# Scores of two heads from one 256-column product over zero-padded keys, in a graph layer on one core

## The chip, the cores and the metric

The kernel runs on one core of one Trainium2 chip, in one launch. The metric is the device time of that launch in microseconds (us). The core's engines each work through a queue of their own and meet at semaphores: TensorE (PE in the profile, with PEld for its weight loads), VectorE (DVE), ScalarE (ACT), GpSimd (POOL) and SyncE (SP, which here only issues DMAs).

## The reference

The kernel computes one layer of a graph network over 8192 nodes of 256 channels and 131072 edges that are sorted by their destination, and a layer norm:

```python
ea  = edge_attr @ w_e + b_e                       # 131072 x 64 -> 256
msg = relu(x[src] + ea)
agg = segment_sum(msg, dst, num_segments=8192)
h_local = bn1(relu((x + agg) @ w1 + b1) @ w2 + b2 + x)
qkv = x.reshape(256, 32, 256) @ in_w.T + in_b      # graphs of 32 nodes
q, k, v = split(qkv), 4 heads of 64 channels each
scores = einsum('bhqd,bhkd->bhqk', q, k) / 8
o = einsum('bhqk,bhkd->bhqd', softmax(scores), v)
h_attn = bn2(o @ out_w.T + out_b + x)
out = h_local + h_attn
out = bn3(out + relu(out @ m_w1 + m_b1) @ m_w2 + m_b2)
return layernorm(x + out)
```

Everything is float32. The change concerns `scores`: for each graph of 32 nodes and each of four heads, the products of 64-channel queries and keys.

## The kernel before

The work has two halves that run side by side.

**Edges.** The 131072 edges are 128 blocks of 1024. For each block POOL issues eight gathers (`gather`, line 205): indirect DMAs that fetch 128 rows of `x` each, into a tile `xs` of four rotating buffers. From block 20 on (`NX`) they fetch from `xb`, a copy of `x` with the edge bias added, which is made in the meantime by DVE (`copy_stream`, line 770) and stored by SP. PE multiplies the edge attributes with `we` (`edge_products`, tile `pe`, two PSUM tiles of two banks each); DVE adds the gathered rows (`edge_messages`, line 280), ACT applies the relu (line 284). PE then sums the messages into windows of nodes (`group_sums`, tile `pw`) and places them (`edge_place`, tile `l`), and DVE adds the result to the transposed node features `xT` (line 351). Before block 20 the bias is added on PE, by a product of the one-row selector `sel` with `be`.

**Nodes.** The nodes are 16 chunks of 512. `attention_front` transposes a chunk, and computes queries and keys (four products of 128 output channels x 512 nodes into PSUM tiles `at`, four banks in all), which ACT moves to the tile `qk` with the bias (line 519). `attention_back` computes the values (`at<-inT,xT`), the scores (lines 541 to 557), the softmax, the weighted values and the output projection. `dense` does the rest, when all edges of the chunk are placed; for the last chunk `dense_rows` does it in pieces of 128 nodes, with `diag` (the identity scaled by the last batch norm `s3`) and `c3row` (its bias as rows). These two are made at block 12, together with the scaling of `mw2`.

In the scores each head has 64 channels, so `qk` holds two heads in its 128 partitions. For each pair of heads and each group of 128 nodes there are two products over 64 partitions each, one for the upper and one for the lower half of the array; their 128 columns go to two different PSUM banks of one `pe` tile, the same tiles that the edge products use:

```python
matmul(two[:, s, a : a + P],
       qk[s * DH : (s + 1) * DH, hh, a : a + P],
       qk[s * DH : (s + 1) * DH, KC + hh, a : a + P], start=True, stop=True)
```

ACT then copies the four diagonal 32 x 32 squares (line 557) to `pr`. The page of the profile counts two instructions for each float32 product.

**Order.** PE's order is that in which the code is written (`manual_schedule`): the loop over blocks asks a planner (`Work`) for pieces of node work, by the costs that the `yield`s give. DVE and ACT follow the written order up to block 24 and are ordered by the compiler's scheduler after that. The gathers are issued in order, and `hold_fetches` lets each wait for a product of PE that the plan puts some 10 us earlier (`AHEAD`; in the tail from block 104 on, by `TAIL_LATE`), so that a PE that falls behind its plan by more than that holds the gathers back.

Of the kernel before, what the change touches and what calls it, by code (L numbers as in the profile page):

```python
# [9 lines left out]
FP = mybir.dt.float32  # L10
I32 = mybir.dt.int32
AF = mybir.ActivationFunctionType
# [6 lines left out]
P = 128  # L19
N, C, E, ED, H, NPG = 8192, 256, 131072, 64, 4, 32  # L20
DH = C // H
KC = C // P
# [11 lines left out]
CH = 512  # L34
NCH = N // CH
BPC = NB // NCH
TN = CH // P
# [7 lines left out]
AHEAD = 10.0  # L45
LATE = 12.0
TAIL_LATE = 9.9
STARTS = [4.8, 7.5, 13.2, 17.0, 20.5]
TE = 1
RS = 1.0 / (1.0 + 1e-5) ** 0.5  # L50
# [27 lines left out]
def gnn_kernel(ctx: ExitStack, tc: tile.TileContext, x, src, dst, edge_attr, w, out):  # L78
    nc = tc.nc

    const = ctx.enter_context(tc.tile_pool(name="const", bufs=1))
# [12 lines left out]
    ident = const.tile([P, P], FP, name="ident")  # L94
# [5 lines left out]
    eps_t = const.tile([P, 1], FP, name="eps_t")  # L100
    nc.vector.memset(eps_t, LN_EPS)

    sel = const.tile([P, P], FP, name="sel")
    nc.vector.memset(sel, 0.0)
    for h in range(2):
        nc.vector.memset(sel[h * ED : h * ED + 1, :], 1.0)
# [9 lines left out]
    be = const.tile([P, C], FP, name="be")  # L116
# [10 lines left out]
    for v in VECS:  # L127
        n = w[v].shape[0] // P
# [3 lines left out]
    def v_(name, i=0, n=1):  # L132
        return vec[:, col[name][0] + i : col[name][0] + i + n]
# [4 lines left out]
    s3 = const.tile([P, KC], FP, name="s3")  # L138
    s12 = const.tile([P, KC], FP, name="s12")
    cA = const.tile([P, KC], FP, name="cA")  # L140
    c3 = const.tile([P, KC], FP, name="c3")
    diag = const.tile([P, KC, P], FP, name="diag")
    c3row = const.tile([P, C], FP, name="c3row")

    fast = ExitStack()
    epool = fast.enter_context(tc.tile_pool(name="edge", bufs=1))
# [3 lines left out]
    def bank():  # L150
        return pps.tile([P, CH], FP, name="at", tag="at", bufs=4)

    def bank2():
        return pps.tile([P, 2, CH], FP, name="pe", tag="pe", bufs=2)
# [10 lines left out]
    def matmul(ps, *args, **kw):  # L165

        mark(ps, nc.tensor.matmul(ps, *args, **kw).ins)  # L167
# [192 lines left out]
    with tc.tile_pool(name="setup", bufs=1) as sp:  # L360
# [15 lines left out]
        for v in VECS:  # L376
            r, n = col[v]
# [7 lines left out]
        for h in range(NH):  # L385
            ps = bank()[:, : TJ * NB].rearrange("p (j s) -> p j s", j=TJ)
# [14 lines left out]


        nc.vector.memset(bd, 0.0)

        def turned(rows, cols, no):
            for o in range(0, no, 2):
# [8 lines left out]
        ps = bank()[:, :nrows]  # L415
# [30 lines left out]
        for h in range(0, NH, 2):  # L446
            ps2 = bank2()
            for i in range(2):
                ps = ps2[:, i, : TJ * NB].rearrange("p (j s) -> p j s", j=TJ)
# [34 lines left out]
        ps = bank()[:, : 2 * NB].rearrange("p (i s) -> p i s", i=2)  # L484
# [10 lines left out]
    def attention_front(n0, st, pool, bank):  # L495
        if "xn" not in st:
            load_nodes(n0, st, pool)
            yield REST
        xn = st["xn"]
        xT = st["xT"] = pool.tile([P, KC, CH], FP, name="xT", tag="xT", bufs=4)  # L500
        hA = st["hA"] = pool.tile([P, KC, CH], FP, name="hA", tag="hA", bufs=4)
        for k in range(KC):
            ps = bank()
            for t in range(TN):
                turn(ps[:, t * P : (t + 1) * P], xn[:, t, k * P : (k + 1) * P], ident)
            nc.scalar.copy(xT[:, k, :], ps)  # L506
            nc.scalar.activation(
                hA[:, k, :], xT[:, k, :], AF.Identity, scale=s12[:, k : k + 1], bias=cA[:, k : k + 1]
            )
        yield 0.9  # L510

        qk = st["qk"] = pool.tile([P, 2 * KC, CH], FP, name="qk", tag="qk")
        for o in range(2 * KC):
            ps = bank()
            for k in range(KC):
                matmul(
                    ps, inT[:, k, o * P : (o + 1) * P], xT[:, k, :], start=(k == 0), stop=(k == KC - 1)
                )
            nc.scalar.activation(qk[:, o, :], ps, AF.Identity, bias=v_("in_b", o))
            st["front"] = o == 2 * KC - 1  # L520
            yield 1.7

    def attention_back(st, pool, bank, bank2):
        xT, hA, qk = st["xT"], st["hA"], st["qk"]
        vn = pool.tile([P, TN, C], FP, name="vn", tag="vn")
        for t0 in range(0, TN, 2):
            ps = bank()
            for t in range(t0, t0 + 2):
                for k in range(KC):
                    matmul(  # L530
                        ps[:, (t - t0) * C : (t - t0 + 1) * C],
                        xT[:, k, t * P : (t + 1) * P],
                        inT[:, k, 2 * C :],
                        start=(k == 0),
                        stop=(k == KC - 1),
                    )
            nc.vector.tensor_copy(vn[:, t0 : t0 + 2, :].rearrange("p t c -> p (t c)"), ps)
            st["v"] = t0 + 2 == TN
            yield 1.7

        pr = pool.tile([P, TN, H, NPG], FP, name="pr", tag="pr")
        for hh in range(H // 2):
            two = bank2()
            for t in range(TN):
                for s in range(2):
                    a = t * P
                    matmul(
                        two[:, s, a : a + P],
                        qk[s * DH : (s + 1) * DH, hh, a : a + P],
                        qk[s * DH : (s + 1) * DH, KC + hh, a : a + P],  # L550
                        start=True,
                        stop=True,
                    )
            two4 = two.rearrange("p s (t k) -> p s t k", t=TN)
            for g in range(GT):
                q = slice(g * NPG, (g + 1) * NPG)
                nc.scalar.copy(pr[q, :, 2 * hh : 2 * hh + 2, :].rearrange("p t s k -> p s t k"), two4[q, :, :, q])
        st["scores"] = True
        yield 1.8
        prf = pr.rearrange("p t h k -> p (t h k)")  # L560
        pr3 = pr.rearrange("p t h k -> p (t h) k")
        mx = pool.tile([P, TN * H], FP, name="mx", tag="mx")
        nc.vector.tensor_reduce(mx, pr3, AX.X, ALU.max)
        parts = [slice(a, a + H) for a in range(0, TN * H, H)]
        for q in parts:
            nc.vector.tensor_sub(pr3[:, q], pr3[:, q], mx[:, q, None].to_broadcast([P, H, NPG]))
        nc.scalar.activation(prf, prf, AF.Exp, scale=1.0 / DH**0.5)
        yield PAUSE if stated[0] else 0.0
        sm = pool.tile([P, TN * H], FP, name="sm", tag="sm")
        nc.vector.tensor_reduce(sm, pr3, AX.X, ALU.add)  # L570
        nc.vector.reciprocal(sm, sm)
        for q in parts:
            nc.vector.tensor_mul(pr3[:, q], pr3[:, q], sm[:, q, None].to_broadcast([P, H, NPG]))

        for g in range(GT):
            q = slice(g * NPG, (g + 1) * NPG)
            nc.vector.transpose(bd[q, :, :, g, :].rearrange("p t h q -> p (t h) q"), pr3[q])  # L577
        yield REST
        oT = pool.tile([P, KC, CH], FP, name="oT", tag="oT")
        for k in range(KC):  # L580
            ps = bank()
            for t in range(TN):
                for s in range(2):
                    h = 2 * k + s
                    matmul(
                        ps[s * DH : (s + 1) * DH, t * P : (t + 1) * P],
                        vn[:, t, h * DH : (h + 1) * DH],
                        bd[:, t, h].rearrange("p g q -> p (g q)"),
                        start=True,
                        stop=True,  # L590
                    )
            nc.scalar.activation(oT[:, k, :], ps, AF.Identity, bias=v_("in_b", 2 * KC + k))
        yield 1.8
        for o in range(KC):
            ps = bank()
            for k in range(KC):
                matmul(
                    ps, outT[:, k, o * P : (o + 1) * P], oT[:, k, :], start=(k == 0), stop=(k == KC - 1)
                )
            nc.vector.scalar_tensor_tensor(  # L600
                hA[:, o, :], ps, s2[:, o : o + 1], hA[:, o, :], op0=ALU.mult, op1=ALU.add
            )
            st["done"] = o == KC - 1
            yield 1.7
# [244 lines left out]
    with tc.manual_schedule(engines={PE}):  # L849
# [9 lines left out]
        for c in range(NCH):  # L859
            st, before, same = chunk[c], chunk[c - 1], chunk[c - 4]  # L860
# [48 lines left out]
        b = 0  # L909
        while b < TAIL:  # L910
# [12 lines left out]

            if b == 12:
                ps = bank()[:, : 2 * C].rearrange("p (i c) -> p i c", i=2)
                for i, cols in enumerate((s3, c3)):
                    for k in range(KC):
                        nc.tensor.transpose(
                            ps[:, i, k * P : (k + 1) * P], cols[:, k : k + 1].to_broadcast([P, P]), ident
                        )  # L930
                nc.vector.tensor_mul(mw2, mw2, ps[:, 0, None, :].to_broadcast([P, 2 * KC, C]))
                nc.vector.tensor_copy(c3row, ps[:, 1, :])
                for k in range(KC):
                    nc.vector.tensor_scalar(diag[:, k], ident, s3[:, k : k + 1], None, ALU.mult)
            if stated[0]:
# [49 lines left out]
        t, l, s = came[b - 2] + 20, b - 2, b - 2  # L985
        p, m = [b, 0], [b, 0]
# [206 lines left out]
```

## Time and profile before

| | |
|---|---|
| median of 3 runs (lowest to highest) | 1314.71 us (1314.67 to 1316.24) |
| the profiled execution | 1313.67 us, span 1311.9 us |
| mean granted TensorE clock | 0.961 |
| PE, PEld, DVE, ACT, POOL busy | 92%, 55%, 61%, 45%, 74% of the span |
| DMA | 240.38 MB in 148926 packets, 183 GB/s |
| PE in the chain that ended last | 69% |

The span runs from the first to the last instruction of the profiled execution; some 2 us of its time lie outside. Rows of a timeline give start, duration, engine, line, operation, what it writes and reads, and in brackets the idle time before it with what ended it. Rows that group instructions give their count, busy time, the mean of one in ns, and the idle time before them. Rows of waits read: who waited for whom, total us, times, the longest in us. PE's spans overlap their successors a little, since the ends of matmuls are modelled: the distance from one start to the next is the better measure.

### The profile page before, as it was taken

How to read it: one execution, taken by the hardware profiler on the slowest of the kernel's cores; microseconds unless marked ns; L12 is line 12 of the kernel's file. 1: busy time of each engine (PE TensorE's matmuls, PEld its weight loads, DVE VectorE, ACT ScalarE, POOL GpSimd, SP SyncE). 2: the span in 40 equal slices, each digit the busy share in tenths (PEclk: the TensorE clock that was granted, in tenths of full speed). 3: DMA queues.
4: the chain of work that ended last, by engine and by line, in shares of the span. 5: the costliest groups of instructions: out<-in, count | busy, mean ns of one | idle time of the engine just before them, and what ended most of it. 6: DMA issues, size and time to landing. Idle time of an engine off the chain costs nothing.

```text
span 1311.9 us, 21686 instructions
## 1 busy us (share of the span) xinstructions
PE 1201.6 (92%) x7671; PEld 725.8 (55%) x7671; DVE 797.5 (61%) x1630; ACT 584.8 (45%) x840; POOL 975.2 (74%) x1032
## 2 busy tenths in 40 slices
PE   5997999999979979799798998989899799999997
PEld 3564555555546555555555555555555555556576
DVE  6675856757447465475745746465474665766563
ACT  2543434545435354253543536444263443545343
POOL 6777777777777777777777777777777777777772
PEclk9998999999989989899898998989999899999999
DMA  9999976766557665665666666566566665757552
GB/s 228 289 315 288 300 210 162 202 159 193 158 157 190 161 187 160 162 183 157 187 170 163 174 168 185 157 183 170 155 187 163 179 182 137 201 154 185 153 153 62
DMA packets 148926, 240.38 MB, mean 183 GB/s; under 512 B 27950, under 2 KB 112204, under 8 KB 148044
## 3 DMA queue, kind: packets, MB, share of 16 engines
q0 software_dynamic: 49152, 134.28, 37.7%
q1 hardware_dynamic: 98572, 104.65, 28.9%
q8 instruction: 62, 1.02, 0.3%
q14 instruction: 52, 0.43, 0.1%
q10 hardware_dynamic: 1088, 0.00, 0.0%
HBM read 222.06 MB, written 16.78 MB: 182 GB/s over the span
## 4 chain that ended last, share of the span: by engine, by line
PE 69%; DMA 10%; DVE 7%; issue 7%; POOL 4%; ACT 1%; SPq 0%; DVEq 0%; POOLq 0%
PE at L167 36%; PE pe L167 17%; PE pw L167 8%; DMA xs<-xb,srci 6%; PE l L167 5%; POOL xs L205 4%; DVE msg L280 3%; DMA xs<-in_x_dram,srci 2%; DVE bd L577 1%; PE at L703 1%; PE at L654 1%; DMA ea<-in_edge_attr_dram 1%; DVE eaT L239 1%; ACT msg L284 1%; PE at L171 1%
## 5 line engine op out<-in xcount | busy, mean ns | idle before, releaser
L205 POOL DMA_INDIRECT xs<-xb,srci x864 | 819.6, 949 | 263.2 <-issue 177.0
L284 ACT ACTIVATE msg<-msg 128x1024 f32<-128x1024 f32 (+1 forms) x259 | 270.7, 1046 | 466.7 <-DVE msg L280 465.6
L280 DVE TENSOR_TENSOR msg<-pe,xs 128x1024 f32<-128x1024 f32 (+1 forms) x259 | 310.3, 1208 | 250.6 <-DMA xs<-xb,srci 179.2
L167 PE MATMUL pe<-we,eaT 64*128 64x256 f32 x2048 | 263.4, 392 | 7.1 <-DVE msg L280 6.8
L167 PEld LDWEIGHTS pe<-we,eaT 64*128 64x128 f32 x2048 | 191.2, 189 | 101.8 <-issue 59.0
L205 POOL DMA_INDIRECT xs<-in_x_dram,srci x144 | 138.4, 961 | 44.1 <-issue 30.2
L167 PE MATMUL pw<-msg,oh 128*32 128x256 f32 x2048 | 136.1, 385 | 2.0 <-ACT msg L284 1.8
L167 PE MATMUL at<-xT,inT 128*128 128x512 f32 x256 | 122.7, 606 | 3.7 <-ACT xT L506 3.7
L167 PE MATMUL at<-hA,mw 128*128 128x512 f32 (+1 forms) x256 | 114.2, 573 | 0.0
L292 DVE TENSOR_TENSOR oh<-iota_n,rel 128x128 f32<-128x128 f32 x256 | 62.3, 281 | 77.6 <-PE pw L167 77.5
L167 PE MATMUL at<-m,mw 128*128 128x512 f32 (+1 forms) x256 | 108.9, 570 | 0.0
L239 DVE STREAM_TRANSPOSE eaT<-ea 128x512 f32<-128x512 f32 x128 | 89.6, 700 | 23.3 <-PE pe L167 19.7
L167 PEld LDWEIGHTS pw<-msg,oh 128*32 128x32 f32 x2048 | 55.1, 109 | 83.1 <-issue 37.6
L167 PE MATMUL pe<-qk 64*128 64x128 f32 x512 | 49.9, 358 | 51.8 <-DVE msg L280 51.8
L167 PE MATMUL l<-oh,ws 128*128 128x160 f32 (+4 forms) x512 | 89.2, 317 | 1.5 <-ACT xT L506 1.5
L167 PEld LDWEIGHTS l<-oh,ws 128*128 128x128 f32 x512 | 77.7, 203 | 22.6 <-issue 17.6
L167 PEld LDWEIGHTS at<-xT,inT 128*128 128x128 f32 x256 | 47.6, 192 | 61.9 <-issue 51.0
L167 PEld LDWEIGHTS pe<-qk 64*128 64x128 f32 x512 | 43.4, 256 | 61.4 <-DVE msg L280 57.3
L167 PEld LDWEIGHTS at<-m,mw 128*128 128x128 f32 x256 | 47.1, 190 | 46.4 <-issue 45.0
L351 DVE TENSOR_TENSOR xT<-l,xT 128x352 f32<-128x352 f32 (+14 forms) x107 | 43.3, 428 | 46.9 <-PE l L167 46.8
L167 PEld LDWEIGHTS at<-hA,mw 128*128 128x128 f32 x256 | 46.2, 190 | 44.6 <-issue 40.3
L635 ACT ACTIVATE m<-at,vec 128x512 f32<-128x512 f32 (+1 forms) x64 | 41.9, 656 | 50.4 <-PE at L167 50.3
(153 smaller groups left out, 1285.8 us busy)
## 6 DMA issues: line engine op xcount, KB each, us to landing
ea<-in_edge_attr_dram SPq DMA_DIRECT2D x512, 128.0 KB
xs<-xb,srci POOLq DMA_INDIRECT x864
xn<-in_x_dram SPq DMA_DIRECT2D x16, 512.0 KB
out_dram<-y SPq DMA_DIRECT2D x14, 512.0 KB
xp<-in_x_dram SPq DMA_DIRECT2D x10, 512.0 KB
xb<-xp SPq DMA_DIRECT2D x10, 512.0 KB
xp<-in_x_dram SPq DMA_DIRECT2D x3, 1024.0 KB
xb<-xp SPq DMA_DIRECT2D x3, 1024.0 KB
```

What stands on the lines that cost most here:

```text
L167: mark(ps, nc.tensor.matmul(ps, *args, **kw).ins)
L171: ins = nc.tensor.transpose(ps, *args).ins
L205: nc.gpsimd.indirect_dma_start(out=xs[:, h, j, :], out_offset=None, in_=x if b < NX else xb[:, :], in_offset=bass.IndirectOffsetOnAxis(ap= ...
L239: nc.vector.transpose(eaT, ea[:, QR:].rearrange("p (g d) -> p g d", d=ED)[:, :, :QR])
L280: nc.vector.tensor_add(msg[:, hs, js].rearrange("p u i c -> p i u c"), pe[:, js, u : u + n, :], xs[:, hs, js].rearrange("p u i c -> p i u c"),
L284: nc.scalar.activation(msg[:, hs, js], msg[:, hs, js], AF.Relu)
L292: nc.vector.tensor_tensor(oh[:, ts], iota_n[:, None, :WN].to_broadcast([P, TB // 2, WN]), rel[:, b, ts, None].to_broadcast([P, TB // 2, WN ...
L351: newest["xT"] = nc.vector.tensor_add(xT, l2[:, :, a - n : z - n], xT).ins
L577: nc.vector.transpose(bd[q, :, :, g, :].rearrange("p t h q -> p (t h) q"), pr3[q])
L635: newest["relu"] = nc.scalar.activation(m1[:, o, :], layer(mw1, KC, o, hA), AF.Relu, bias=v_("m_b1", o)).ins
L654: nc.tensor.transpose(ps[:wt, t - t2, k * P : (k + 1) * P], zT[:, k, t * P : t * P + wt], ident)
L703: nc.tensor.matmul(ps[i], wt[:, k, o * P : (o + 1) * P], act[:, k, :], start=(k == 0), stop=(k == nk - 1))
```

## The change

There are two parts.

1. **Scores.** The keys no longer go to `qk` but to a new tile `kz` of 2 x 2 x 512 columns, which is cleared once at the start. For each pair of heads it holds two copies of the 512 columns: in the first only the partitions of the one head are ever written, in the second only those of the other, so the rest stays zero. ACT therefore moves each key product in two pieces of 64 partitions x 512. One product over all 128 partitions, with 128 queries as weights and 256 columns of `kz`, then gives the scores of both heads: 8 products a chunk in place of 16, each of twice the columns. `qk` shrinks to the queries.
2. **The last layer's matrix.** `diag` now lies in the memory of `be` and `c3row` in that of `sel`, which are read until block 19; so they are made at block 40 (`LATE_ROWS`) rather than at block 12, with a PSUM bank and two transposes there.

On PE nothing else moves but the two transposes of the second part. At chunk 15, the last (`pe` is the PSUM tile, `hA`, `inT` and `m_` belong to node work, `eaT` and `msg` to edges), the order was

```order
L167 MATMUL at<-hA,mw_94 128x512 x2
L167 MATMUL at<-inT,xT 128x256 x4
L167 MATMUL at<-hA,mw_94 128x512 x2
L167 MATMUL pe<-qk 128x128 x16
L167 MATMUL pw<-msg,oh 32x256 x8
L167 MATMUL pe<-we,eaT 128x256 x8
```

and is now

```order
L169 MATMUL at<-hA,mw_94 128x512 x2
L169 MATMUL at<-inT,xT 128x256 x4
L169 MATMUL at<-hA,mw_94 128x512 x2
L169 MATMUL pe<-kz,qk 128x256 x8
L169 MATMUL pw<-msg,oh 32x256 x8
L169 MATMUL pe<-we,eaT 128x256 x8
```

The scores keep their place between the node work and the sums of the edges. On ACT, the keys of the same chunk were moved by these rows

```order
L284 ACTIVATE msg<-msg 128x1024
L635 ACTIVATE m_8816<-at,vec 128x512
L519 ACTIVATE qk<-at,vec 128x512
L327 COPY ws<-pw 128x256
L635 ACTIVATE m_8816<-at,vec 128x512
L284 ACTIVATE msg<-msg 128x1024 x2
L519 ACTIVATE qk<-at,vec 128x512
L327 COPY ws<-pw 128x256
```

and now are by these

```order
L286 ACTIVATE msg<-msg 128x1024
L636 ACTIVATE m_8727<-at,vec 128x512
L527 ACTIVATE kz<-at,vec 64x512 x2
L329 COPY ws<-pw 128x256
L636 ACTIVATE m_8727<-at,vec 128x512
L286 ACTIVATE msg<-msg 128x1024 x2
L527 ACTIVATE kz<-at,vec 64x512 x2
L329 COPY ws<-pw 128x256
```

Two instructions stand where one stood, ahead of the same copies and relus. At the start of DVE's queue the order was

```order
L101 MEMSET eps_t 128x1
L104 MEMSET sel 128x128
L403 MEMSET bd 128x2048
L106 MEMSET sel 1x128 x2
L384 COPY srcf<-srci_r 128x1024
```

and is now

```order
L102 MEMSET eps_t 128x1
L106 MEMSET c3row 128x128
L405 MEMSET bd 128x2048
L108 MEMSET c3row 1x128 x2
L406 MEMSET kz 128x2048
L386 COPY srcf<-srci_r 128x1024
```

The clearing of `kz` stands just ahead of the first instruction that needs loaded data. POOL's order and the semaphores that it names are unchanged; on SP one load of a weight matrix stands behind one store to `xb` instead of ahead of it.

```diff
+LATE_ROWS = 40
...
-    sel = const.tile([P, P], FP, name="sel")
+    c3row = const.tile([P, C], FP, name="c3row")
+    sel = c3row[:, :P]
...
-    diag = const.tile([P, KC, P], FP, name="diag")
-    c3row = const.tile([P, C], FP, name="c3row")
+    diag = be.rearrange("p (k n) -> p k n", k=KC)
+    kz = const.tile([P, KC, 2, CH], FP, name="kz")
...
         nc.vector.memset(bd, 0.0)
+        nc.vector.memset(kz, 0.0)
...
-        qk = st["qk"] = pool.tile([P, 2 * KC, CH], FP, name="qk", tag="qk")
+        qk = st["qk"] = pool.tile([P, KC, CH], FP, name="qk", tag="qk")
...
-            nc.scalar.activation(qk[:, o, :], ps, AF.Identity, bias=v_("in_b", o))
+            if o < KC:
+                nc.scalar.activation(qk[:, o, :], ps, AF.Identity, bias=v_("in_b", o))
+            else:
+                for s in range(2):
+                    rows = slice(s * DH, (s + 1) * DH)
+                    nc.scalar.activation(kz[rows, o - KC, s, :], ps[rows], AF.Identity, bias=v_("in_b", o)[rows])
...
+            two4 = two.rearrange("p i (t s k) -> p (i t) s k", t=TN // 2, s=2)
             for t in range(TN):
-                for s in range(2):
-                    a = t * P
-                    matmul(
-                        two[:, s, a : a + P],
-                        qk[s * DH : (s + 1) * DH, hh, a : a + P],
-                        qk[s * DH : (s + 1) * DH, KC + hh, a : a + P],
-                        start=True,
-                        stop=True,
-                    )
-            two4 = two.rearrange("p s (t k) -> p s t k", t=TN)
+                a = t * P
+                matmul(two4[:, t], qk[:, hh, a : a + P], kz[:, hh, :, a : a + P], start=True, stop=True)
             for g in range(GT):
                 q = slice(g * NPG, (g + 1) * NPG)
-                nc.scalar.copy(pr[q, :, 2 * hh : 2 * hh + 2, :].rearrange("p t s k -> p s t k"), two4[q, :, :, q])
+                nc.scalar.copy(pr[q, :, 2 * hh : 2 * hh + 2, :], two4[q, :, :, q])
...
             if b == 12:
...
-                for i, cols in enumerate((s3, c3)):
+                for i, cols in enumerate((s3,)):
...
-                nc.vector.tensor_copy(c3row, ps[:, 1, :])
+            if b == LATE_ROWS:
+                ps = bank()[:, :C]
+                for k in range(KC):
+                    nc.tensor.transpose(
+                        ps[:, k * P : (k + 1) * P], c3[:, k : k + 1].to_broadcast([P, P]), ident
+                    )
+                nc.vector.tensor_copy(c3row, ps)
                 for k in range(KC):
                     nc.vector.tensor_scalar(diag[:, k], ident, s3[:, k : k + 1], None, ALU.mult)
```

## The prediction

> **What bounds the kernel now.** I read the busy times first, then who waits on each engine, then the stretches around the scores. By busy time PE looks like the bound:
>
> ```profile
> PE 1201.6 (92%) x7671; PEld 725.8 (55%) x7671; DVE 797.5 (61%) x1630; ACT 584.8 (45%) x840; POOL 975.2 (74%) x1032
> ```
>
> The waits say otherwise. First POOL's waits and gathers, then the two largest data waits of DVE and PE:
>
> ```profile
> POOL xs L205 <- issue: 214.1, 695, 2.6
> POOL xs L205 <- PE at L167: 25.6, 84, 0.3
> L205 POOL DMA_INDIRECT xs<-xb,srci x864: 942/946/1122, 207.8 to 1289.4; - x173
> L205 POOL DMA_INDIRECT xs<-in_x_dram,srcd x16: 942/946/1493, 4.2 to 24.0; - x16
> DVE msg L280 <- DMA xs<-xb,srci: 179.2, 83, 4.7
> PE pe L167 <- DVE msg L280: 64.6, 25, 5.2
> ```
>
> 1024 gathers start between 4.2 and 1289.4 us: (1289.4 - 4.2) / 1023 = 1.256 us each, and 0.946 of work plus the 0.3 that every start costs is 1.25. So POOL issues gathers without a break; the 26% in which it is not busy is 1024 times 0.3. What comes behind follows it: DVE's additions wait 179 us for gathered rows, and PE 65 us for DVE to empty the `pe` tiles. PE's 92% is work that fits in beside the gathers. The end is 4.2 + 1285 + 22.5 us of tail, and only three things can move it: the first gather, the pace of the gathers (through contention, or through PE falling behind its plan until a gather is held), and the tail.
>
> **The scores on PE.** The group of the first score products, of those of chunks 5 and 15, and two groups of 256-column products that use all 128 partitions:
>
> ```profile
> 55.44 2.06 PE L167 MATMUL pe<-qk 64*128 64x128 f32 x32
> 57.43 1.13 PE L167 MATMUL l<-oh,ws 128*128 128x96 f32 x8
> 387.61 2.08 PE L167 MATMUL pe<-qk 64*128 64x128 f32 x16 [5.24 <-DVE msg L280]
> 391.17 2.08 PE L167 MATMUL pe<-qk 64*128 64x128 f32 x16 [1.48 <-DVE msg L280]
> 393.17 2.50 PE L167 MATMUL l<-oh,ws 128*128 128x160 f32 x8
> 1165.81 2.06 PE L167 MATMUL pe<-qk 64*128 64x128 f32 x32
> 1167.80 1.07 PE L167 MATMUL pw<-msg,oh 128*32 128x256 f32 x16
> 1162.28 1.89 PE L167 MATMUL at<-inT,xT 128*128 128x256 f32 x8
> 1164.00 1.88 PE L167 MATMUL at<-hA,mw 128*128 128x512 f32 x4
> 53.52 1.99 PE L167 MATMUL at<-inT,xT 128*128 128x256 f32 x8
> 386.00:396.00 10.00, 6.91 (x43) 6.35 (x44) 3.36 (x4) 4.90 (x10) 7.56 (x9) 0.50 0.57 154
> ```
>
> Before, a chunk's 32 instructions take 57.43 - 55.44 = 1.99 us, 0.124 us for each pair: the two half-array products run side by side. The change has 16 instructions of 256 columns over the whole array. Such rows cost (1164.00 - 1162.28) / 8 = 0.215 us each, or (55.44 - 53.52) / 8 = 0.24. I take 0.215, since that group too stands among products of the whole array: 16 x 0.215 = 3.44 us, so +1.45 a chunk; at 0.24 it is +1.85, and if the two were to overlap better than these rows, not below 0. Seven chunks (0 to 4, 14, 15) run so without a break: +10.2 us of PE. In chunks 5 to 13 a group comes in two halves with a wait between (1.48 us in the rows), at a granted clock of 0.50: each half takes 2.08 and would take 8 x 0.43 = 3.44. The first half's growth of 1.36 lies inside the wait; the second half's does not: 9 x 1.36 = 12.2. PE has +22.4 us in all.
>
> [...]
>
> **What hides it.** PE's waits in four stretches: blocks 4 to 21, then to 1100 us, then around chunk 14, and from chunk 15 to the end; and the gather that had the least room behind its product in the tail:
>
> ```profile
> PE pe L167 <- DVE msg L280: 6.0, 2, 5.1
> PE at L167 <- ACT xT L506: 3.7, 4, 2.0
> PE pe L167 <- DVE msg L280: 55.1, 20, 5.2
> PE pe L167 <- DVE msg L280: 2.8, 1, 2.8
> PE at L703 <- DVE xT L351: 2.0, 3, 1.1
> PE pe L167 <- DVE msg L280: 0.6, 2, 0.4
> 1127.23 2.00 PE L167 MATMUL pe<-we,eaT 64*128 64x256 f32 x16
> 1132.57 0.95 POOL L205 DMA_INDIRECT xs<-xb,srci  x1 [0.31 <-issue]
> ```
>
> The order of PE is fixed, so a longer group makes it late until a wait for gathered rows is met, and that wait then is shorter. Chunks 0 to 3 add 5.8 us against waits of 9.7; chunks 4 to 13 add 13.7 against 55; chunk 14 adds 1.45 and meets a wait of 2.8; chunk 15 adds 1.45 and meets 2.0 + 0.6. A gather feels none of it unless PE is later than the gather's own room. Matching each gather's semaphore value with the product that reaches it, the least room after block 3 is that of the gather at 1132.57, whose product is the last of the group of edge products that ends at 1129.23: 3.3 us. A lateness of at most 1.85 (3.7 if two chunks' add up, which the 2.8 us wait between them prevents) stays near or under it. So the pace of the gathers keeps, and of chunk 15's 1.45 us I leave 0.3 to the end, because the waits behind it (1.1, and a few of 0.2 to 0.4) are small and partly DVE's own backlog; bounds 0 and +1.45.
>
> If that cover went, the second thing late would be the edge products behind the scores, and with them the `xs` buffers.
>
> **The keys on ACT, and the copies.**
>
> ```profile
> L519 ACT ACTIVATE qk<-at,vec 128x512 f32<-128x512 f32 x64 | 43.7, 683 | 40.2 <-PE at L167 39.8
> L557 ACT COPY pr<-pe 32x256 f32<-32x256 f32 x128 | 46.2, 361 | 14.9 <-PE pe L167 13.3
> L327 ACT COPY ws<-pw 128x256 f32<-128x256 f32 x26 | 9.7, 372 | 30.1 <-PE pw L167 29.9
> PE pw L167 <- ACT msg L284: 1.8, 1, 1.8
> ```
>
> The two copies show that 32 partitions cost what 128 do at the same 256 elements (361 and 372 ns), so a piece of 64 x 512 costs about the 683 ns of a whole one. Two more a chunk are 32 x 0.683 = +21.9 us, ACT at 607 us, 46%. Behind each stand relus and the copies of `pw`; they come 0.7 us later, and PE waited for a relu once in the middle stretch (1.8 us). I cost it at 0, hidden by PE's same waits for gathers. The copies of the scores read as many elements as before: 0.
>
> **The clearing of `kz`.** The start of DVE and POOL:
>
> ```profile
> 1.42 1.76 DVE L403 MEMSET bd<- 128x2048 f32 x1 [0.38 <-issue]
> 3.15 0.39 DVE L106 MEMSET sel<- 1x128 f32 x2
> 4.24 1.10 POOL L205 DMA_INDIRECT xs<-in_x_dram,srcd  x1 [2.63 <-issue]
> 7.41 1.20 DVE L384 CAST srcf<-srci_r 128x1024 f32<-128x1024 int32 x1 [3.87 <-DMA srci_r<-in_src_dram]
> 17.25 1.49 POOL L205 DMA_INDIRECT xs<-in_x_dram,srcd  x1 [0.30 <-issue]
> 17.54 1.08 DVE L436 CAST dstf<-dsti_r 128x1024 f32<-128x1024 int32 x1 [1.68 <-DMA dsti_r<-in_dst_dram]
> 19.05 0.95 POOL L205 DMA_INDIRECT xs<-in_x_dram,srcd  x1 [0.30 <-issue]
> 18.65 1.22 DVE L441 TENSOR_REDUCE lo<-dstf 128x4 f32<-128x1024 f32 x1
> ```
>
> It has the size of `bd`'s, 1.76 us, and fits into DVE's wait of 3.87 for the edge indices: 0 on DVE. But from 3.5 to 5.3 us it lies beside the first gather. A cast that lay beside a gather made it 1.49 long, +0.54; the reduction beside the gather at 19.05 left it at 0.95. A delay of the first gather delays the end by as much, so the bounds are 0 and +1.1 (the gather's whole 1.10 blocked). I take 0, by the reduction, as the cast is the only kind of these that stretched one.
>
> **The rest, together.** Block 12 loses two transposes and three short DVE instructions, block 40 gets them; there the middle stretch's waits of 55 us hide them, and the one PSUM bank more. The swap on SP is one load and one store, neither an edge load: 0.
>
> **The sum.** The profiled execution took 1313.67 us, 1.04 below the median. 1313.67 + 0.3 (tail) + 0 + 0 = 1313.97; against the median of 1314.71 that is 1315.0.
>
> **Rivals.**
>
> *PE's lateness reaches the gathers (slower).* It decides in the tail, at the room of 3.3 us at 1132.57 and at the end. The point is an instruction of 0.33 us rather than 0.215: then a group grows by 16 x 0.33 - 1.99 = 3.3. At 0.43, the price of half clock, it grows by 4.9: gathers are held some 1.6 us, and about 3 of chunk 15's 4.9 are left at the end: 1319 to 1320. For it: PE is busy almost throughout the tail. Against it: the rows of 0.215 in that same stretch. [...]
>
> *ACT's order becomes the wait (slower).* Relus come 0.7 us later twice a chunk, 1.4 us each; if PE met them every time, 16 x 1.4 = 22 us, 1337; if in the tail alone, +1.4, which is no change by the bound below. Against it: ACT is idle 55%, and one such wait stands in the rows.
>
> *The gathers get faster (faster).* Only a shorter pace could do it. At the rows' least duration throughout, 942 for 946 ns, 1024 gathers would gain 4.1 us: 1310.6. But the change takes just three short DVE instructions from beside them, at block 12, and puts them back at block 40; nothing in the rows says that the pace would move.
>
> **How the numbers follow.** A measurement of this kernel can tell about 0.2%, 2.6 us, from no change (its three runs span 1.6). My forecast, hidden work with an end between 1312.8 and 1317.3, has 0.70; PE's lateness 0.17; ACT's order 0.06; a faster pace or a gain that I see no cause for 0.07. Slower by over 0.2% holds 0.23, faster 0.07. The range of 8 in 10 takes the forecast with its bounds (+1.1 clearing, +1.45 tail, and the runs' own spread) and the nearer part of PE's lateness: 1312.8 to 1320.
>
> **What would show it.** Scores as 16 instructions of 0.215 us, 3.4 us a chunk, where they run unbroken; PE busy up by some 20 us and its waits for DVE's additions down by as much; ACT busy up by 22; gathers still 1.256 us apart, the last at 1289 to 1291; the first gather still of 1.1 us. I am wrong if POOL shows waits of more than 0.3 us for PE in blocks 104 to 126, if the last gather starts after 1292, or if the tail behind it grows beyond 24 us.

## The result, and the profile after

The changed kernel takes 1318.68 us (median of 21 runs, 1316.32 to 1322.13), the kernel before, run beside it, 1315.66 us (21 runs, 1313.81 to 1317.27): a ratio of 1.0024, interval 1.0017 to 1.0030, 3.0 us slower. A later comparison gave 1.0020 (1.0009 to 1.0030). That lies inside the range of 1312.8 to 1320 and 3.7 us above the forecast of 1315.0. By the bound of 0.2% it is just slower, the side that had 0.23, and not the case that had 0.70. Of the 3.7 us, 0.95 are the kernel before itself, whose median over 21 runs is that much above the one of three that the forecast started from.

The page after, span and engines:

```profile
span 1317.1 us, 21218 instructions
PE 1218.0 (92%) x7415; PEld 733.4 (56%) x7415; DVE 798.4 (61%) x1631; ACT 608.8 (46%) x872; POOL 977.1 (74%) x1032
```

PE is busy 16.4 us more than before, ACT 24.0 more; DVE and POOL as before. The parts of the change come first by tile (count, shortest, median and longest in ns, first and last start in us) and by line, the scores before and after; then the scores of chunk 15 and what follows them:

```profile
L406 DVE MEMSET kz<- x1: 1765/1765/1765, 4.0 to 4.0; 128x2048 f32 x1
L527 ACT ACTIVATE kz<-at,vec 64x512 f32<-64x512 f32 x64 | 43.5, 680 | 24.6 <-PE at L169 24.1
L558 ACT COPY pr<-pe 32x256 f32<-32x256 f32 x128 | 46.3, 361 | 24.2 <-PE pe L169 23.0
L167 PE MATMUL pe<-qk 64*128 64x128 f32 x512 | 49.9, 358 | 51.8 <-DVE msg L280 51.8
L169 PE MATMUL pe<-kz,qk 128*128 128x256 f32 x256 | 77.4, 465 | 40.9 <-DVE msg L282 40.9
1170.31 3.62 PE L169 MATMUL pe<-kz,qk 128*128 128x256 f32 x16
1173.86 1.07 PE L169 MATMUL pw<-msg,oh 128*32 128x256 f32 x16
```

1173.86 - 1170.31 = 3.55 us for 16 instructions, 0.22 each, where the old group took 1.99. All score products together keep PE busy for 77.4 us in place of 49.9. The waits, of PE first, then of POOL:

```profile
PE pe L169 <- DVE msg L282: 53.3, 23, 5.8
PE at L169 <- ACT xT L509: 11.0, 7, 3.1
POOL xs L207 <- issue: 214.1, 695, 2.7
POOL xs L207 <- PE at L169: 22.4, 71, 0.9
```

PE waits 11 us less for DVE's additions (64.6 before), and POOL is held for PE beyond its usual 0.3 us at 82 us only, by 0.8 in all. So what PE has to do more held almost no gather. Yet the last of them is late, as the view of the tile `xs` tells:

```profile
L207 POOL DMA_INDIRECT xs<-xb,srci x864: 942/946/1782, 208.0 to 1291.9; - x173
```

Before, the longest was 1122 ns and the last start 1289.4. The end comes 1317.1 - 1291.9 = 25.2 us behind the last gather, where it was 22.5. The profiled execution is 5.2 us longer than before's: 2.5 us of later gathers and 2.7 of tail.

**Where the gathers lost it.** Around the subtractions of the softmax of chunk 6 (L567, four instructions on DVE). POOL and DVE after:

```profile
477.86 0.95 POOL L207 DMA_INDIRECT xs<-xb,srci  x1 [0.30 <-PE at L169]
479.12 1.78 POOL L207 DMA_INDIRECT xs<-xb,srci  x1 [0.30 <-DVE mv L664]
481.20 1.07 POOL L207 DMA_INDIRECT xs<-xb,srci  x1 [0.31 <-issue]
479.00 0.27 DVE L333 TENSOR_SCALAR oh<-iota_n,wrow 128x160 f32<-128x160 f32 x1
479.19 0.89 DVE L567 TENSOR_TENSOR pr<-pr,mx 128x128 f32<-128x128 f32 x4
```

And the same place before:

```profile
479.80 0.95 POOL L205 DMA_INDIRECT xs<-xb,srci  x1 [0.30 <-issue]
481.05 0.95 POOL L205 DMA_INDIRECT xs<-xb,srci  x1 [0.30 <-issue]
479.88 0.27 DVE L331 TENSOR_SCALAR oh<-iota_n,wrow 128x160 f32<-128x160 f32 x1
480.07 0.89 DVE L566 TENSOR_TENSOR pr<-pr,mx 128x128 f32<-128x128 f32 x4
```

After, the gather begins 0.07 us ahead of the subtractions and ends 0.82 us behind their end (480.08 to 480.90): as if nearly all of its work were done after them. Before, it began 0.27 us ahead of them and took 0.95. DVE does the same work in both; only the moment has moved. In the trace after, four gathers between 320 and 962 us take 1.37, 1.78, 1.69 and 1.49 us; three of them begin beside these subtractions, one beside a one-hot comparison (L294). From the 200th gather on, the gathers spend 4.5 us in all above 0.946 each, before 2.2: these 2.3 us are nearly the whole 2.5 by which the last one is late.

How such a gather ends is the same everywhere. The 14 traces of this study hold 46 gathers behind the 200th that took 1.26 us or more, and every one of them ends 0.82 us (0.816 to 0.825) behind the last of an unbroken row of two-input instructions on DVE. Counted are those with both inputs in SBUF; DVE's additions, which read `pe` from PSUM, are not among them. In 45 cases these are the subtractions, in some with a one-hot comparison right behind them; in one it is two such comparisons alone.

**Where the tail lost it.** The window from 1085 to 1100 us: length, busy time of each engine with the count of instructions, granted clock, DMA share, GB/s; before, then after:

```profile
1085.00:1100.00 15.00, 14.85 (x94) 9.69 (x95) 7.28 (x14) 4.69 (x8) 11.35 (x13) 1.00 0.50 141
```

```profile
1085.00:1100.00 15.00, 12.95 (x68) 8.10 (x68) 6.49 (x11) 6.74 (x9) 11.39 (x12) 0.89 0.51 142
1088.51 3.53 PE L169 MATMUL pe<-we,eaT 64*128 64x256 f32 x16
```

A stretch at half clock (mean granted clock 0.54 from 1088.5 to 1092, 0.89 in the whole window, 1.00 before) fell on the edge products there: 3.53 us for a group that takes 2.00 elsewhere. Behind chunk 15's scores PE stands at 1173.86 and stood at 1167.80: 6.1 us later, where the gathers are 2.5 later. Of PE's own 3.5, 2.9 are the longer scores of chunks 14 and 15 and 1.5 the half clock, less what the waits gave back.

### The profile page after: what moved, and what is told of

Same layout as the page of the kernel before. It is cut to its first block, busy times and chain, and to the rows that moved or that the text cites. A ratio compares the mean times of both kernels' runs of the same rounds, so it can differ in the third digit from the quotient of the medians.

```text
span 1317.1 us, 21218 instructions
## 1 busy us (share of the span) xinstructions
PE 1218.0 (92%) x7415; PEld 733.4 (56%) x7415; DVE 798.4 (61%) x1631; ACT 608.8 (46%) x872; POOL 977.1 (74%) x1032
## 4 chain that ended last, share of the span: by engine, by line
PE 67%; DMA 12%; DVE 9%; issue 6%; POOL 4%; ACT 1%; SPq 0%; DVEq 0%; POOLq 0%; ACTq 0%
PE at L169 33%; PE pe L169 19%; PE pw L169 7%; DMA xs<-xb,srci 7%; PE l L169 4%; POOL xs L207 4%; DMA xs<-in_x_dram,srci 3%; DVE msg L282 3%; DVE bd L578 2%; PE at L704 1%; DMA xn<-in_x_dram 1%; ACT msg L286 1%; DVE eaT L241 1%; DMA ea<-in_edge_attr_dram 1%; PE at L655 1%
## 5 line engine op out<-in xcount | busy, mean ns | idle before, releaser
L169 PE MATMUL pe<-we,eaT 64*128 64x256 f32 x2048 | 266.5, 396 | 7.6 <-DVE msg L282 7.6
L169 PE MATMUL pe<-kz,qk 128*128 128x256 f32 x256 | 77.4, 465 | 40.9 <-DVE msg L282 40.9
L294 DVE TENSOR_TENSOR oh<-iota_n,rel 128x128 f32<-128x128 f32 x256 | 62.3, 280 | 70.1 <-PE pw L169 69.5
L169 PEld LDWEIGHTS pe<-kz,qk 128*128 128x128 f32 x256 | 59.0, 237 | 59.2 <-DVE msg L282 47.6
L169 PEld LDWEIGHTS l<-oh,ws 128*128 128x128 f32 x512 | 72.6, 191 | 21.8 <-issue 17.1
L169 PE MATMUL l<-oh,ws 128*128 128x160 f32 (+4 forms) x512 | 81.6, 299 | 1.5 <-ACT xT L509 1.5
```

The costliest lines, as they stand in the source:

```text
L294: nc.vector.tensor_tensor(oh[:, ts], iota_n[:, None, :WN].to_broadcast([P, TB // 2, WN]), rel[:, b, ts, None].to_broadcast([P, TB // 2, WN ...
```

## The experiments

Two theories stood against each other at first. *Tail*: the end pays for the longer scores of the last two chunks, because the waits behind them are PE's own and do not shrink. *Gathers*: the loss is in the gathers stretched beside DVE.

One circumstance must be known for the first eight runs. In their two sessions every kernel took 19 to 20% longer, the one before too (1562 and 1581 us), and POOL was held for some 240 to 260 us in all, over half of it for PE by the profile's account. In the third session the first session's chip ran the kernel before in 1315 us. Numbers are compared within a session only; the last section shows what differed.

### First session: the longer scores, undone in parts

In the chunks of a set `HALF`, the scores come again from 16 pairs of half-array products, over the same tiles:

```
+            if st.get("c") in HALF:
+                for t in range(TN):
+                    for s in range(2):
+                        a = t * P
+                        half = slice(s * DH, (s + 1) * DH)
+                        matmul(
+                            two[:, s, a : a + P], qk[half, hh, a : a + P], kz[half, hh, s, a : a + P],
+                            start=True, stop=True,
+                        )
...
+                continue
...
+            st["c"] = c
```

With `HALF` all 16 chunks only the clearing, the split keys and the moves at blocks 12 and 40 are left of the change.

> The kernel after, but every chunk's scores are 16 half-array products again, each over 64 partitions of qk and of the copy of kz that belongs to its head; the padded tile, its clearing, the keys moved in halves and the late matrix stay. If the time comes from the wider products on PE (the tail theory or any other theory on the products), this is as fast as the kernel before, ratio 0.999 to 1.001. If it comes from ACT's extra instructions or the clearing, it stays at 1.0024, some 3 us slower.

Measured: 1563.21 us, 0.9989 of the kernel before (0.9968 to 1.0009).

`HALF` = chunks 14 and 15:

> The kernel after, with half-array products in chunks 14 and 15 alone; chunks 0 to 13 keep the 256-column products. Tail theory: PE has nothing to give after block 108, so the 1.5 us by which each of the last two groups grew go to the end, and all others are hidden: ratio 1.000 to 1.001 (0 to 1 us slower than before). Gather theory (the shifted work of the earlier chunks lets DVE stretch more gathers): the last gather still starts 2 us or more later, ratio 1.0015 to 1.002.

Measured: 1563.17 us, 1.0003 (0.9988 to 1.0018).

`HALF` = chunks 0 to 13:

> The reverse: 256-column products in chunks 14 and 15 alone, half-array products in chunks 0 to 13. Tail theory: nearly all of the difference is back, ratio 1.0018 to 1.0024 (2.2 to 3 us), the last gather within 1 us of before, and the tail behind it 2 to 3 us longer. Gather theory: 1.000 to 1.001.

Measured: 1561.20 us, 0.9992 (0.9980 to 1.0005).

The change itself in that session:

> The kernel after itself, for a second profiled execution and as the measure on the same chip: ratio 1.0024. If the four gathers of 1.4 to 1.8 us that its first trace showed belong to the change, they stand at the same places again; if they are chance, others do or none.

Measured: 1557.92 us, 0.9960 (0.9942 to 0.9978): faster there, by 4.4 us, where 1.0024 was expected. Stretched gathers stand in this trace too, but seven of them, and most at other chunks. POOL's waits in it:

```profile
POOL xs L207 <- issue: 230.8, 731, 2.7
POOL xs L207 <- remote: 102.5, 70, 3.3
POOL xs L207 <- PE at L169: 95.7, 82, 5.0
POOL xs L207 <- PE pe L169: 68.8, 61, 3.7
```

Gathers were held up to 5.0 us for PE: another bound than the one this study is about. None of the four expectations for a kernel whose gathers run unbroken could be tested, and the parts do not add up either (the version with 14 of 16 chunks changed shows nothing of the 0.4%). What follows is only that the shares of the change cannot be read here.

### Second session: the tail alone, and the subtractions taken out

Chunks 14 and 15 in halves, and the converse, once more:

> The changed kernel, but chunks 14 and 15 again form their scores from 16 pairs of half-array products (of the same tiles qk and kz). Tail theory (the end pays for the longer scores of the last two chunks, since the waits behind them are PE's own loops and don't shorten): 1.5 to 2.7 us less than the change, so 0 to +1 us against the kernel before where the change is +3. Gather theory (the loss is in gathers stretched beside VectorE, and in what the new order does to them): no gain, +2.5 to +3 us as the change. On a chip where PE already stalls and the kernels take 1560 us, as in the first runs, neither theory separates; there I expect a difference below 0.3 % either way.

> The other half: chunks 0 to 13 form their scores from pairs of half-array products, only chunks 14 and 15 from 256 columns. Tail theory: nearly the whole loss of the change is here, +2 to +3 us against the kernel before. Gather theory: chunks 14 and 15 alone cost no more than 1 us. On a chip where PE stalls, within 0.3 % of the kernel before.

Measured: 1580.58 us, 0.9989 (0.9965 to 1.0013), and 1580.27 us, 0.9996 (0.9972 to 1.0021). As expected of such a session, they tell nothing apart.

The score products of chunks 14 and 15 issued twice:

```
+                for _ in range(2 if st.get("c", 0) >= 14 else 1):
+                    matmul(two4[:, t], qk[:, hh, a : a + P], kz[:, hh, :, a : a + P], start=True, stop=True)
```

> The changed kernel, with the 16 score products of chunks 14 and 15 issued twice (the second overwrites the first with the same values): 2 x 3.44 = 6.9 us more on PE in the tail. Tail theory: nearly all of it comes out at the end, 5.5 to 7 us over the change (+8.5 to +10 us over the kernel before where the change is +3). Rival, the waits in the tail absorb (the prediction's step): at most 3 us over the change. On a chip where PE stalls PE is late in any case, and the tail theory's 5.5 to 7 us should show there too, on top of whatever the change does there.

Measured: 1586.87 us, 1.0035 (1.0012 to 1.0058): 6.0 us over the kernel before, for 6.9 us of products. The change was not run beside them; the two variants above stand at -0.3 and -0.7 us against before. By the medians little absorbed the products (the interval leaves 1.9 to 9.2 us), but PE held the gathers here in any case.

The softmax without its maximum:

```
-        mx = pool.tile([P, TN * H], FP, name="mx", tag="mx")
-        nc.vector.tensor_reduce(mx, pr3, AX.X, ALU.max)
...
-            nc.vector.tensor_sub(pr3[:, q], pr3[:, q], mx[:, q, None].to_broadcast([P, H, NPG]))
```

> The changed kernel without the maximum of the softmax (one reduction and four subtractions of VectorE fewer a chunk, 16 x 1.6 = 26 us of VectorE; the exponentials are taken of the scores themselves, which leaves out the usual guard against overflow). Theory that gathers are stretched beside back-to-back VectorE operations with two inputs from SBUF: the gathers of 1.7 us at chunks 6, 10 and 12 are gone, and the last gather starts 1.5 to 2 us earlier than with the change; with the shorter chain of the last chunk 0.5 to 2 us more, so 2 to 4 us under the change. Rival, the stretches come from something else beside them: gathers of over 1.3 us stay as many, and the gain is below 1.5 us. On a chip where PE stalls I expect 1 to 5 us less, from the shorter chains alone.

Measured: 1578.67 us, 0.9975 (0.9953 to 0.9998). The gathers of this run, and those of the change in the first session:

```profile
L207 POOL DMA_INDIRECT xs<-xb,srci x864: 942/949/1052, 255.6 to 1549.3; - x173
```

```profile
L207 POOL DMA_INDIRECT xs<-xb,srci x864: 943/949/1542, 253.3 to 1536.6; - x173
```

In the change's run seven gathers behind the 200th took 1.27 us or more, all of them beside the subtractions; without the subtractions none took more than 1.05. Alone that is no proof, since of the six other runs of these sessions, all with the subtractions, two had no such gather either; and PE set the end here. But the six sort by their scores. The three with 256 columns in chunks 0 to 13 (`half_last2`, `half_last2_b`, `twice_last2`) had 8, 6 and 7 such gathers, the three with half-array products there (`half_all`, `full_last2`, `full_last2_b`) 0, 0 and 2.

### Third session: gathers unbroken again

The change once more:

> The changed kernel itself once more, as the measure for the next two. Where PE keeps its plan (the profile shows POOL held for 0 to 1 us in all), +3 us against the kernel before. Where PE stalls and POOL is held for some 250 us, as in the runs so far, 0 to 6 us less than before.

Measured: 1317.90 us against 1315.24, 1.0020 (1.0009 to 1.0030). Its gathers, and the same window as above:

```profile
L207 POOL DMA_INDIRECT xs<-xb,srci x864: 942/947/1827, 207.6 to 1293.6; - x173
1085.00:1100.00 15.00, 12.33 (x70) 7.20 (x72) 6.64 (x11) 6.71 (x10) 11.34 (x13) 1.00 0.56 146
```

This execution (span 1316.2) divides the loss otherwise: the last gather is 4.2 us later than before, and the tail is 22.6 us, as before (22.5). Five gathers between 478 and 963 us took 1.57 to 1.83, all beside the subtractions; from the 200th on, the gathers spend 6.6 us above 0.946 each, 4.4 more than before. The granted clock was 1.00 throughout this window (0.89 in the first trace of the change), and the later gathers left PE waits enough: it stands 5.2 us later behind chunk 15 (1173.03), only 1.0 more than the gathers there.

The score products of chunks 14 and 15 four times, and those of chunks 7 and 8 four times, 20.6 us of PE each:

```
+                for _ in range(4 if st.get("c") in (14, 15) else 1):
+                    matmul(two4[:, t], qk[:, hh, a : a + P], kz[:, hh, :, a : a + P], start=True, stop=True)
```

> The changed kernel with the score products of chunks 14 and 15 issued four times (the last has the same values): 2 x 3 x 3.44 = 20.6 us more on PE, near the end. Tail theory: 17 to 20.6 us over the change. Waits in the tail absorb (the prediction's step): under 8 us over the change.

> The same 20.6 us more on PE, but in chunks 7 and 8. Where PE keeps its plan, PE's waits of some 5 us a block for gathered rows take it back: 0 to 4 us over the change (the gathers may be held for a moment, since 10.3 us come at once). Where PE stalls and is itself what holds the gathers, nothing takes it back: 15 to 21 us over the change, as much as near the end.

Measured: 1339.75 us (ratio to before 1.0187, 1.0174 to 1.0200), 21.9 us over the change, a little above even the tail theory's range; and 1321.73 us (1.0054, 1.0039 to 1.0069), 3.8 over it, as expected. POOL near the end, with the scores of the last chunks four times:

```profile
1113.26 0.94 POOL L207 DMA_INDIRECT xs<-xb,srci  x1 [0.30 <-issue]
1120.15 0.95 POOL L207 DMA_INDIRECT xs<-xb,srci  x1 [5.95 <-PE pe L169]
1123.59 0.94 POOL L207 DMA_INDIRECT xs<-xb,srci  x1 [2.49 <-PE at L169]
1182.40 0.95 POOL L207 DMA_INDIRECT xs<-xb,srci  x1 [0.30 <-issue]
1194.03 0.94 POOL L207 DMA_INDIRECT xs<-xb,srci  x1 [10.67 <-PE pe L169]
```

In the middle, 16.8 of 20.6 us do not reach the end. PE's waits for DVE's additions are 9.3 us shorter there (43.4 where the change's run beside it has 52.7), and PE ran 53 us at half clock instead of 67 (mean granted clock 0.981 and 0.975). What is left is mainly one gather held for 3.1 us, because 10.3 us come at once. Near the end all of it reaches the gathers: the holds above the usual 0.3 add up to 20.2 us.

The room behind the products, 3.3 us at its least before the change, is nearly used up in the first trace of the change. The gather at 1181.50 there starts 0.6 us after the product for which the same gather is held when the last scores run four times; before, it had 3.7. So in that trace 2.9 us more in the last two chunks, with the half clock, just fit. In the later trace of the change, where the gathers were late themselves, it had 3.0.

The version that the readings favoured, chunks 14 and 15 in halves and no maximum (without the usual guard against overflow):

> The version that the readings so far favour: 256 columns in chunks 0 to 13, pairs of half-array products in chunks 14 and 15, and no maximum in the softmax (which leaves out the usual guard against overflow). Where PE keeps its plan: 1 to 3 us less than the kernel before (no gather above 1.2 us after the first 140, a shorter chain in the last chunk). Where PE stalls: 2 to 6 us less than before, as the kernel without the maximum. The rival, that the stretched gathers have another cause: gathers of 1.27 us and more at regular places, as in the runs with the maximum.

Measured: 1314.57 us, 0.9996 of the kernel before (0.9986 to 1.0006), 3.3 us under the change.

```profile
L208 POOL DMA_INDIRECT xs<-xb,srci x864: 942/946/1075, 208.6 to 1290.3; - x173
```

No gather is stretched, the last starts 3.3 us earlier than in the change's run beside it, and the loss is gone; the gain of 1 to 3 us over the kernel before is not there. It takes away both causes at once, so it does not say how the 3 us divide.

**The moments, side by side.** When the gather began, counted from the first subtraction of chunks 5 to 10 and 12, and what it took, both in us and worked out from the timelines:

```
chunk   before        after         third session  first session
                      (the change)  (the change)   (the change)
  5     +0.32 0.98    +0.62 1.09    -0.20 0.95     +0.44 1.27
  6     -0.26 0.95    -0.07 1.78    -0.12 1.82     +0.44 1.28
  7     +0.32 0.98    -0.20 0.95    -0.12 1.83     +0.44 1.28
  8     -0.23 0.95    +0.32 0.98    -0.10 1.81     +0.44 1.28
  9     +0.32 0.98    -0.20 0.96    +0.78 0.94     +0.44 1.28
 10     -0.35 0.95    +0.02 1.69    +0.14 1.57     +0.44 1.27
 12     -0.35 0.95    +0.42 1.49    +0.21 1.70     -0.17 1.07
```

The 14 that grew by more than 0.3 us all began between 0.12 us ahead of the first subtraction and 0.44 into the 0.89 that the four last. (0.44 + 1.27 - 0.89, 0.02 + 1.69 - 0.89 and -0.12 + 1.82 - 0.89 all give an end 0.81 to 0.82 us behind them; in chunk 12 it is 1.02, because a one-hot comparison follows there.) Before, none began in that stretch but the three at +0.32, an offset that costs nothing after either. Equal offsets in chunk after chunk suggest that the subtractions stand in a fixed step to the gathers, which a change can shift as a whole. Over all sessions, each of the eight traces with 256-column products in chunks 0 to 13 and the subtractions has 2 to 8 stretched gathers; of the four with half-array products there, the kernel before among them, three have none and one has two. In the other chunks some gathers begin in the same stretch and are not stretched; what distinguishes them, and +0.32, stays open.

## Why the prediction was right or wrong

- **What bounds the kernel: right.** Gathers without a break set the time: of 20.6 us of products added in the middle, 3.8 showed. One reading of the sum is loose: 1024 times 0.3 is 307 us or 23%; the rest of POOL's 26% is mainly the 22.5 us of tail and the first 4.2.
- **The scores on PE: right.** 0.22 us an instruction, 3.45 to 3.55 us a chunk where unbroken, against 3.44. That PE's total grew by 16.4 where 22.4 was forecast is two errors against each other, and so partly luck. The score products alone took 27.5 us more (49.9 to 77.4). The seven unbroken chunks account for 10.4, as forecast. In chunks 5 to 13 the second halves grew by 1.9 us in all and not by 12.2, since six of the nine ran at a mean granted clock of 0.86 to 1.00, where before all nine had 0.50; the first halves, which the sum left out as hidden, grew by 13.8. All else on PE took 11 us less, at 80 us of half clock in place of 104 (mean granted clock 0.970 and 0.961).
- **Keys on ACT, copies, clearing: right.** 680 ns a piece, 361 ns a copy, ACT +24.0 (forecast +21.9). The clearing lies from 4.0 to 5.8 us beside the first gather, which took 1.10 as before. For the moves at blocks 12 and 40, counted as 0, no gather's hold speaks against it, but no run has them alone.
- **What hides it: the mechanism right.** No gather behind block 8 was held by PE. But the adding up of two chunks, which the wait of 2.8 us between them was to prevent, happened: PE's waits for DVE behind 1100 us only fell from 3.5 to 2.7 us, and one gather's room shrank from 3.7 to 0.6 us in the first trace.
- **"Of chunk 15's 1.45 us I leave 0.3 to the end": mis-sized in one execution.** The tail behind the last gather grew by 0.1 us in one trace and by 2.7 in the other. The waits of the last layers measure 2.0 and 0.4 us in both, as before: they absorbed nothing. In the one trace the gathers were 4.2 us late themselves, so PE's lateness did not show; in the other 1.5 us of half clock came on top, a term that the sum did not have.
- **"So the pace of the gathers keeps": this step failed.** The last gather came 2.5 and 4.2 us later, and waits for PE hardly enter into it (0.8 us in one trace, none in the other). The prediction asked only whether a gather is held, and of what DVE does beside it only which instructions are added or removed. With the change the subtractions of the softmax stood at other moments against the gathers, and some gathers then grew by 0.3 to 0.9 us: 2.3 us in all in one trace, 4.4 in the other. The rival on the pace looked at a gain alone.
- **Its own signs** said so: "the last gather after 1292" came true in one trace (1293.6), "a tail beyond 24 us" in the other (25.2). That the time still fell inside the range is luck in this part: the range was widened for the clearing, the tail and PE's lateness, and not for gathers that take longer.

How the 3 us of the medians divide is not settled. The two traces of the change are 5.2 and 4.3 us longer than the one of before, which was itself 2.0 us under the median of its 21 runs and below the lowest of them; what its usual executions spend more is not recorded. That gathers wait for DVE's subtractions is shown by the 0.82 us in all 46 cases, by the table and by the two runs without them, where none of the 864 later gathers passes 1.08 us. That the longer scores of chunks 0 to 13 bring the subtractions into the gathers is what the count of twelve traces says (2 to 8 against 0, 0, 0 and 2); by which waits they do so is argued from the order of the work, not shown. Where gathers are unbroken, the half-array side of this count is the one trace of the kernel before, and no version with chunks 14 and 15 in halves and the subtractions kept was run, so the tail's part of the medians stays open.

## What to carry to other kernels

Where an engine issues transfers without a break, ask not only what holds it but what runs beside it, and when: a change that adds nothing to an engine can still move its work into the wrong moment of another's (here DVE was busy for 797.5 us before and 798.4 after, and single gathers took up to 1.83 us instead of 0.946). Work put into waits is free only up to the least room on the path (here 3.3 us; of 20.6 us more, 3.8 reached the end from the middle and 21.9 from the last two chunks), and the room is shared by all that comes after, so several small additions near the end count as one. One trace gives one outcome of such coincidences: two of the same kernel divided the same loss in opposite ways, so a cause of 3 us needs a second trace before it is named.

## What was not expected of the hardware

**Gathers and DVE's two-input instructions.** The gather at 479.12 took 1.78 us, three in the later run of the change 1.81 to 1.83, against 0.946. All 46 stretched gathers end 0.82 us behind the last of a row of DVE instructions with both inputs in SBUF, as if they did most of their 0.946 only then. By what the one makes the other wait, no run shows. In the table the step lies between 0.20 us ahead of the subtractions, where a gather took 0.95, and 0.12 ahead, where it took 1.82. Why some chunks escape at the same offsets no trace shows.

**Sessions in which everything takes 19% longer.** In the first session PE issued instructions of one group, without a wait of their own, 0.70 or 1.40 us apart instead of 0.2 to 0.45. Rows of the change's run there:

```profile
64.09 0.59 PE L169 MATMUL pw<-msg,oh 128*32 128x256 f32 x1 [1.03 <-issue]
65.49 0.59 PE L169 MATMUL pw<-msg,oh 128*32 128x256 f32 x1 [0.81 <-issue]
66.89 1.34 PE L169 MATMUL pw<-msg,oh 128*32 128x256 f32 x2 [0.81 <-issue]
```

Some 160 to 190 weight loads in each of the eight traces stand over 0.65 us behind the one before in their group, 76 to 94 us beyond a pitch of 0.45; in the six traces of the other sessions it is 3 to 9. That alone is not the whole of it: the kernel before took 247 us longer in the first session than in the third. The eight also hold only 8,800 to 9,600 semaphore records, the six 28,800 to 28,900; so who released whom is less certain in the eight. Missing records and paced instructions come together here; whether the one brings the other, or both have another cause, no run shows, so it stays open.
